# Transposed z and experts' products one piece later in the sequence, mask additions with a near due time

## The chip, the cores and the metric

The kernel runs on one core of a Trainium2 chip. The metric is the device time of one execution in microseconds (us). Of the kernel before, three timed executions and one profiled execution are at hand. The engines are named as in the profile: PE is TensorE's matmul side (PEld its weight loads), DVE is VectorE, ACT is ScalarE, POOL is GpSimd, SP is SyncE, which issues most DMAs.

## The reference, cut to what matters

A block of a transformer on x of shape (2, 1024, 1024): local attention on a convolved input, then a linear layer with four active low-rank experts and a gate.

```python
x = x + attn(layernorm(x))       # conv 3 -> q, k, v; 16 blocks of 128 tokens, 16 heads of 64
    # scores = where(causal, q k / 8, -1e9); p = softmax(scores); o = p v; o wo; @ proj_w + proj_b
xn = layernorm(x)
y = xn @ W_base.T + b_base
z = einsum(xn, A[active])                        # 4 experts, rank 8
alpha = softmax(log(prior + eps) + router(xn))   # over the 4 active experts
x = x + y + sum_e alpha_e * 2 * (z_e @ B_e)
```

## The kernel before, in words

Three stages follow each other. In the **convolution** (to about 233 us) x is normalised, transposed and convolved. In the **attention stage** (233 to about 490 us) a unit i is a pair of heads in a chunk of 512 tokens, 32 units in all, and step K of the loop (L1382) handles two of them. The **dense stage** (from about 523 us) handles the 2048 tokens in 16 pieces n of 128. The end of the attention stage, the first projections and the rounding of the dense weights overlap between 480 and 526 us; I call this the passage.

Products keep close to full precision with pairs of rounded numbers: `three` (L136 to L140) does hi x hi, hi x lo and lo x hi, so nearly all matmuls have line 140. A "hi" part is a cast on ACT, a "lo" part a subtraction on DVE.

The order of the instructions on each engine is decided when the program is built. Every operation is an `Op` (L269) with an engine, an assumed cost, a due time, a lead, operations that it comes after, and the places in pools that it needs and gives back. `trace` (L289) plays the plan: on each engine it takes, among the operations that can start, the first one by due time, and the one that can start at once before the others. An operation may start at most its lead ahead of its due time. The due time of PE's operations is the running sum of their costs (`at[0]`), in the order in which the plan's functions are called; those of other engines are set relative to it. The result is a fixed order: each engine works through its queue in order, and an instruction that waits holds up all that are queued behind it on that engine. A change of one due time can so move operations on all engines.

Names of operations, used below (i a unit, n a piece):

- Attention: Q.i, V.G.b (products for queries and keys, and values), q, v (their copies from PSUM; v with even b on ACT, L864, odd b on DVE, L862), S.i (scores, `scores`, L887), k.i (two mask additions, `masked`, L903, on DVE), x.i (maximum, L917), e.i (exponentials on ACT in two halves of four, L922), r.i (reciprocal, L929), n.i (normalisation on POOL, L933), T.i (transposed probabilities, L940), t.i (their copies, L948 on DVE and L950 on ACT), O.i (probabilities x values, L957), h.i and l.i (hi and lo of it, L971 and L978), W.i (product with wo).
- yj, yk, yl, y: steps that put together the convolved tokens on DVE (L559 to L589), which read and write SBUF.
- Dense stage: X.n loads x (L1069), POOL adds the projection's bias to it (L1072). P.n is the projection in two halves (`project`, L1074), the residual is added on DVE (L1087); then statistics (L132, L134, L1092), 1/std on POOL (L1097), normalised xn.n (L1102), TX.n (its transposition in two halves, L1109), xT.n hi and lo (L1116 on ACT, L1120 on DVE). Y.n.k.dc is a third k of the columns times one eighth dc of the rows of the weights. Columns 0 to 35 of k = 0 hold z and the router's logits; from them `plan_gate` makes the gate (L1151 to L1175) after Y.n.0.7. Z.n transposes gate x z (L1179), ACT copies it to zT (L1183), E.n.k adds the experts' products to the same banks (L1193), DVE adds them to x (L1200), and when all three thirds are added, SP stores the piece (L1206).
- Weight parts rl, wz (L1052, L1060): rounding of the dense weights on DVE in the passage.

Pools: `m` is PSUM, 8 banks, which every product from Q to Z takes (S takes two) and the copy or addition that reads it last gives back; for S it is the mask additions. `a4` (11 tiles) holds the probabilities, their transposes, oT, the x tiles, xn and xT (two tiles). A tile of it goes to the operation that asks next, the one given back longest ago first.

Around the change, the loop over the pieces (L1460) calls for n = 1 to 15: TX of n+1, P of n+2, for n = 1 the z and experts of piece 0, the first third of the columns, the gate, the second third, the last third, then z and experts of piece n itself. The last piece has its own ending. Mask additions (L1249) have a due time of 11 us before T.i of their unit, and a lead of 40 us.

Of the kernel before, what the change touches and what calls it, by code (L numbers as in the profile page):

```python
# [39 lines left out]
def preln_block_kernel(  # L40
# [592 lines left out]
    DVE, ACT, PE, DMA = "DVE", "ACT", "PE", "DMA"  # L633
# [4 lines left out]
    loaded, gs, gone = {}, {}, {}  # L638
# [69 lines left out]
    last, ready = None, {}  # L708
# [5 lines left out]
    for q, (v, n, dc) in enumerate(units):  # L714
# [6 lines left out]
        due = at[0]  # L721
# [3 lines left out]
        for i in range(2):  # L725
            d = dc + i
# [4 lines left out]
            for c in range(NCC):  # L731
                after = [last, side, ready[v, d]]
                if v == 5 and n == 0 and d == 0:
                    after.append(gone[0, max(0, c - 1)])
                last = Op(
                    PE, HALF / NCC, at[0], 6.0, after, partial(multiply_unit, q, i, c), lag=0.0
                )
# [28 lines left out]
    def product(v, d, c, side):  # L766
        after = [last, side, ready[v, d]]
        if d == 0:
            after.append(gone[v - 1 if v > 1 else 5, max(0, c - 1)])
        at[0] += HALF / 3  # L770
        return Op(
            PE, HALF / 3, at[0] - HALF / 3, 6.0, after, partial(multiply, v, d, c), lag=0.0
        )
# [7 lines left out]
    for v, dc in [(v, dc) for v in (1, 2, 3) for dc in range(0, NDC, 2)] + [(4, 0), (4, 2)]:  # L781
# [6 lines left out]
        for d in (dc, dc + 1):  # L788
            begin_chunk(v, d, at[0])
            for c in range(NCC):  # L790
                last = product(v, d, c, side)
# [14 lines left out]
    for c in range(NCC):  # L806
# [4 lines left out]
        for d in range(NDC // 2, NDC):  # L811
            last = product(4, d, c, sides[d - d % 2])
# [313 lines left out]
    def cut(n, k):  # L1126
        return (LAST_CUTS if n == len(gs) - 1 else CUTS)[k]
# [88 lines left out]
    gs = [ch * NB + b for ch in (2, 3, 0, 1) for b in range(NB)]  # L1216
    d = {}

    def pe(key, takes, after, f, lead=8.0, need=("m",), give=()):
        d[key] = Op(PE, takes, at[0], lead, [d.get(a) for a in after], f, need=need, give=give)  # L1220
        at[0] += takes
        return d[key]

    def op(key, e, takes, due, after, f, lead=14.0, **kw):
        d[key] = Op(e, takes, due, lead, [d[a] for a in after if a in d], f, **kw)
        return d[key]
# [9 lines left out]
    def plan_v(G, b):  # L1236
        ch, g = divmod(G, 2)
        pe(("V", G, b), MM, [("y", ch, 4), ("y", ch, 5)], partial(values, G, b),
           give=("t4",) * 2 if g == 1 and b == NB - 1 else ())
        op(("v", G, b), *((DVE, 0.6) if b % 2 else (ACT, 0.55)), at[0], [("V", G, b), ("v", G, 0)],  # L1240
           partial(values_out, G, b), need=("vh",) if b == 0 else (), give=("m",))
# [4 lines left out]

    def plan_softmax(i, due):
        for j in range(2):
            op(("k", i, j), DVE, 0.69, due - 11.0 + 0.7 * j, [("S", i), ("k", i, j - 1)],  # L1249
               partial(masked, i, j), need=("a4",) if j == 0 else (), give=("m",), lead=40.0)  # L1250
        op(("x", i), DVE, 1.21, due - 9.5, [("k", i, 0), ("k", i, 1)], partial(maximum, i),
           lead=40.0)
        for j in range(2):
            op(("e", i, j), ACT, 1.6, due - 8.0 + 1.6 * j, [("x", i)], partial(exponentials, i, j),
               lead=40.0)
        op(("r", i), DVE, 0.2, due - 4.0, [("e", i, 0), ("e", i, 1)], partial(reciprocal, i),
           lead=40.0)
        op(("n", i), POOL, 2.3, due - 3.7, [("r", i)], partial(normalized, i), lead=40.0)
# [9 lines left out]
    def plan_o(i):  # L1268
        pe(("O", i), 0.9, [("t", i, 0), ("t", i, 1)] + [("v", i // 4, b) for b in range(NB)],
           partial(attend, i), give=("a4",) + (("vh",) if i % 4 == 3 else ()))  # L1270
        op(("h", i), ACT, 0.6, at[0] + 1.0, [("O", i)], partial(attended_hi, i), need=("a4",))
        op(("l", i), DVE, 0.7, at[0] + 2.0, [("h", i)], partial(attended_lo, i), give=("m",))
# [15 lines left out]
    def plan_tokens(ch, c, due):  # L1288
        k = (ch, c)
        op(("yd", *k), DMA, 1.0, due - 12.0, [("W", 0)] if ch == 1 and c < 0 else [],  # L1290
           partial(tokens_load, ch, c, ml), lead=6.0, lag=3.3, need=("ml",))
        op(("yj", *k), DVE, 0.75, due - 5.0, [("yd", *k)], partial(tokens_join, ch, c, 0),
           need=("t2", "t2"))
        op(("yk", *k), DVE, 1.0, due - 4.0, [("yj", *k)], partial(tokens_join, ch, c, 1))
        op(("yl", *k), DVE, 0.95, due - 3.0, [("yk", *k)], partial(tokens_join, ch, c, 2),
           give=("ml", "t2"))
        op(("yh", *k), ACT, 0.6, due - 1.8, [("yl", *k)], partial(tokens_hi, ch, c),
           need=("t4",))
        op(("y", *k), DVE, 0.64, due - 0.8, [("yh", *k)], partial(tokens_lo, ch, c),
           give=("t2",))  # L1300
# [34 lines left out]
    def plan_tx(n):  # L1335
        g = gs[n]
        for h in range(2):
            pe(("TX", n, h), 0.44, [("xn", n)], partial(transpose_x, g, h),
               give=("a4",) if h else ())
            op(("xh", n, h), ACT, 0.55, at[0] + 0.5, [("TX", n, h), ("xh", n, 0)],  # L1340
               partial(x_hi, g, h),
               need=("a4",) * 2 if h == 0 else ())
            op(("xl", n, h), DVE, 0.65, at[0] + 1.2, [("xh", n, h)], partial(x_lo, g, h),
               give=("m",))

    def after_dense(n, k, dc):
        return [("xl", n, dc // 4), ("rl", "wb", dc, 0), ("rl", "wb", dc, 1), ("wz", dc, 1)] + (
            [("Y", n, k, dc - 1)] if dc else [])

    def plan_dense(n, k, dcs):  # L1350
        a, b = cut(n, k)
        for dc in dcs:
            pe(("Y", n, k, dc), 3 * (b - a) * 0.000454, after_dense(n, k, dc),
               partial(dense, n, k, [dc]), need=("m",) if dc == 0 else (),
               give=("a4",) * 2 if (k, dc) == (2, NDC - 1) else ())

    def plan_gate(n):
        g = gs[n]
        op(("g0", n), DVE, 0.4, at[0] + 0.5, [("Y", n, 0, NDC - 1)], partial(gate_logits, g))
        op(("g1", n), ACT, 0.3, at[0] + 1.0, [("g0", n)], partial(gate_exp, g))  # L1360
        op(("g2", n), DVE, 1.25, at[0] + 2.0, [("g1", n)], partial(gate, g))

    def plan_z(n):
        pe(("Z", n), 0.1, [("g2", n)], partial(transpose_z, gs[n]))
        op(("z", n), ACT, 0.2, at[0], [("Z", n)], partial(z_out, gs[n]), give=("m",))

    def plan_e(n, k, last):
        a, b = cut(n, k)
        pe(("E", n, k), (b - a) * 0.00046, [("z", n), ("Y", n, k, NDC - 1)], partial(experts, n, k),
           need=())  # L1370
        op(("a", n, k), DVE, 0.55, at[0] + 0.5, [("E", n, k)], partial(add_y, n, k), give=("m",))
        if last:
            op(("o", n, k), DMA, 0.7, at[0] + 1.0, [("a", n, k)], partial(store, n, k))
        elif k == 2:
            op(("o", n), DMA, 1.4, at[0] + 1.0, [("a", n, j) for j in range(3)], partial(store, n),
               lag=3.3, give=("a4",))

    PAIRS = NI // 2
    for i in range(2):
        plan_q(i)  # L1380
    pools = ["ml", "t2", "ml", "t2"]
    for K in range(PAIRS):  # L1382
        a, b = 2 * K, 2 * K + 1
# [3 lines left out]
        if K > 1:  # L1387
            for i in (a - 4, b - 4):
                plan_o(i)
        if K + 1 < PAIRS:  # L1390
            for i in (a + 2, b + 2):
# [4 lines left out]

        for v in (range(2 * (K % 2), 2 * (K % 2) + 2) if K < PAIRS - 2 else range(NB)):
            if K < PAIRS - 1:
                plan_v(K // 2, v)
# [12 lines left out]
        if K % 4 == 0 and K:  # L1412
            plan_tokens(ch - 1, 5, t0 + 6.0)
        if K == PAIRS - 4:
            op(("pb",), DMA, 1.4, t0 + 8.0, [], load_projb, lag=3.0, need=("t4",))
            op(("bb0",), DVE, 1.0, t0 + 1.0, [], load_bb, lag=5.0, need=("t4", "t4"))
            op(("bb1",), ACT, 2.3, t0 + 9.0, [("bb0",)], round_bb)
            op(("bb2",), DVE, 1.2, t0 + 12.0, [("bb1",)], finish_bb, give=("t4", "t4"))
        if K == PAIRS - 3:
            for k, (wc, h) in enumerate([(wc, h) for wc in range(NWC) for h in range(2)]):  # L1420
# [35 lines left out]
        for k in range(3):  # L1456
            plan_dense(0, k, [dc])
    plan_gate(0)
    done = 0
    for n in range(1, len(gs)):  # L1460
        last = n == len(gs) - 1

        if n + 1 < len(gs):
            plan_tx(n + 1) if n + 1 > 1 else None
        if n + 2 < len(gs):
            plan_p(n + 2)
        if n == 1:
            plan_z(0)
            for k in range(3):
                plan_e(0, k, False)  # L1470
        plan_dense(n, 0, range(NDC))
        plan_gate(n)
        plan_dense(n, 1, range(NDC))
        if not last:
            plan_dense(n, 2, range(NDC))
            plan_z(n)
            for k in range(3):
                plan_e(n, k, False)
        else:
            plan_z(n)  # L1480
            plan_dense(n, 2, range(3))
            for k in range(2):
                plan_e(n, k, True)
            plan_dense(n, 2, range(3, NDC))
            plan_e(n, 2, True)
# [72 lines left out]
```

## Time and profile before

| what | us |
| --- | --- |
| three timed executions | 785.03, 786.18, 786.32 |
| their median | 786.18 |
| the profiled execution | 783.39 |
| its span from the first to the last instruction | 781.1 |
| mean granted TensorE clock | 0.995 |
| PE busy in 500 to 540 us | 38.06 of 40 |
| PE busy in 540 to 580 us | 37.57 of 40 |
| PE busy in 620 to 660 us | 40.00 of 40 |
| DVE busy in 260 to 300 us | 39.10 of 40 |

How to read it: a line of a timeline is the start (us from the span's start), the busy time, engine, source line, operation, output<-inputs, shapes and number of instructions; in square brackets stands the idle time of the engine before it and who ended it. A line of the waits has the total, the number and the longest. Spans on POOL are rough, and PE's ends are modelled, so its work is better taken from the starts of successive matmuls. The chain of waits follows the work back from the end; its lines are start, duration and what ran.

### The profile page before, as it was taken

The numbers are of one execution on the slowest core, as the hardware profiler recorded it, in microseconds if no ns is written. First come the engines' busy times: TensorE is split into PE (matmuls) and PEld (weight loads), VectorE is DVE, ScalarE is ACT, GpSimd is POOL, SyncE is SP. The second block draws the span as 40 slices with busy tenths as digits, with TensorE's granted clock in tenths as the row PEclk, the third lists the DMA queues.
The fourth block names the chain that finished last, engine by engine and source line by source line (L and its number), as shares of the span: only waits on it lengthen the run. The fifth ranks groups of instructions, "written<-read, shape, count | busy, mean of one in ns | idle before, by whom it ended". The sixth has DMA issues, their size and how long they took to land.

```text
span 781.1 us, 13001 instructions
## 1 busy us (share of the span) xinstructions
PE 755.7 (97%) x4928; PEld 675.3 (86%) x4928; DVE 544.9 (70%) x1034; ACT 386.5 (49%) x1006; POOL 158.0 (20%) x138
## 2 busy tenths in 40 slices
PE   6999999999999999999999999999899999999995
PEld 6999978888888888888888888879899999999995
DVE  7788899889766998877786767995445544345431
ACT  6887346364836887777686977740011001010110
POOL 3224222110000311131112215231111121111100
PEclk9999999999999999999999999999999999999998
DMA  9837993994832111021032113310123212221111
GB/s 344 350 102 222 235 270 101 310 257 126 257 114 76 41 42 41 34 83 41 21 96 82 41 55 117 105 69 19 63 77 107 70 62 90 96 71 60 36 47 54
DMA packets 48118, 87.58 MB, mean 112 GB/s; under 512 B 3591, under 2 KB 22807, under 8 KB 48057
## 3 DMA queue, kind: packets, MB, share of 16 engines
q1 hardware_dynamic: 44328, 76.76, 28.6%
q0 software_dynamic: 3728, 10.00, 7.1%
q8 instruction: 38, 0.62, 0.3%
q14 instruction: 24, 0.19, 0.1%
HBM read 66.83 MB, written 19.92 MB: 111 GB/s over the span
## 4 chain that ended last, share of the span: by engine, by line
PE 62%; DVE 19%; DMA 13%; ACT 3%; issue 2%; POOL 1%; SPq 0%; ACTq 0%; DVEq 0%; POOLq 0%
PE pm L140 22%; DMA out<-xr 12%; PE pq L140 10%; PE py L140 9%; PE pw L140 4%; PE pv L140 4%; PE s L893 3%; PE po L957 3%; PE pt L940 2%; DVE lnst_b L132 2%; DVE xr L1087 2%; PE pp L140 2%; ACT p L922 2%; DVE xT L1120 1%; PE tr L385 1%
## 5 line engine op out<-in xcount | busy, mean ns | idle before, releaser
L140 PE MATMUL pm<-v,u 128*128 128x256 f32 (+1 forms) x1152 | 204.9, 339 | 5.7 <-ACT v L473 3.4
L140 PEld LDWEIGHTS pm<-v,u 128*128 128x128 f32 x1152 | 179.3, 191 | 28.9 <-ACT v L473 3.6
L140 PE MATMUL py<-wb,xT 128*128 128x354 f32 (+3 forms) x576 | 113.2, 327 | 0.0
L933 POOL TENSOR_TENSOR p<-p,rs 128x1024 f32<-128x1024 f32 x32 | 61.6, 1927 | 244.6 <-DVE rs L929 221.8
L140 PE MATMUL py<-wb_wr,xT 128*128 128x354 f32 (+3 forms) x576 | 108.8, 324 | 0.0
L922 ACT ACTIVATE p<-p,nmx 128x128 f32<-128x128 f32 x256 | 99.3, 392 | 3.5 <-DVE nmx L917 3.5
L140 PEld LDWEIGHTS py<-wb_wr,xT 128*128 128x128 f32 x576 | 96.2, 188 | 2.0
L140 PEld LDWEIGHTS py<-wb,xT 128*128 128x128 f32 x576 | 95.0, 189 | 0.2
L140 PE MATMUL pq<-yt,wqk 128*128 128x512 f32 x384 | 94.3, 399 | 0.9 <-DVE p L908 0.9
L140 PEld LDWEIGHTS pq<-yt,wqk 128*128 128x128 f32 x384 | 70.8, 188 | 19.3 <-DVE p L908 1.7
L1157 ACT ACTIVATE al<-lg,nm 128x4 f32<-128x4 f32 x16 | 4.8, 298 | 143.7 <-DVE nm L1152 143.7
L1072 POOL TENSOR_TENSOR xr<-xr,projb 128x1024 f32<-128x1024 f32 x16 | 39.1, 2443 | 165.1 <-DMA xr<-in_x 130.0
L1120 DVE TENSOR_TENSOR xT<-trx,xT 128x512 fp32r<-128x512 f32 x32 | 21.6, 686 | 44.0 <-ACT xT L1116 39.0
L922 ACT ACTIVATION_READ_ACCUMULATOR p<-p,nmx 128x1 f32 x256 | 48.9, 191 | 0.0
L140 PE MATMUL pw<-oT,wot 128*128 128x512 f32 x192 | 47.6, 396 | 0.0
L908 DVE TENSOR_TENSOR p<-s,mask 128x512 f32<-128x512 f32 x64 | 42.1, 681 | 7.2 <-PE s L893 7.1
L140 PE MATMUL pv<-wvt,yt 128*128 128x512 f32 x192 | 46.6, 392 | 0.0
L140 PEld LDWEIGHTS pw<-oT,wot 128*128 128x128 f32 x192 | 35.9, 188 | 8.6 <-DVE oT L978 0.2
L140 PEld LDWEIGHTS pv<-wvt,yt 128*128 128x128 f32 x192 | 36.1, 188 | 8.2
L1116 ACT CAST xT<-trx 128x512 fp32r<-128x512 f32 x32 | 17.7, 590 | 51.1 <-DMA out<-xr 45.5
L1200 DVE TENSOR_TENSOR xr<-py,xr 128x318 f32<-128x318 f32 (+5 forms) x48 | 23.9, 507 | 26.3 <-PE py L1193 26.3
L917 DVE TENSOR_REDUCE nmx<-p 128x8 f32<-128x1024 f32 x32 | 38.6, 1208 | 0.4
(161 smaller groups left out, 1188.2 us busy)
## 6 DMA issues: line engine op xcount, KB each, us to landing
g<-in_conv_w SPq DMA_DIRECT2D x48, 384.0 KB
mdr<-m SPq DMA_DIRECT2D x36, 256.0 KB
g<-in_conv_w POOLq DMA_DIRECT2D x24, 384.0 KB, 7.7
xt<-in_x SPq DMA_DIRECT2D x16, 512.0 KB
xr<-in_x SPq DMA_DIRECT2D x16, 512.0 KB
out<-xr SPq DMA_DIRECT2D x15, 512.0 KB
ml<-mdr SPq DMA_DIRECT2D x18, 384.0 KB
raw_wb<-in_w_base SPq DMA_DIRECT2D x16, 256.0 KB
```

The costliest lines, as they stand in the source:

```text
L132: nc.vector.bn_stats(st[:, h, :], src[:, ts(h, D // 2)])
L140: nc.tensor.matmul(ps, l[a], r[b], start=first and i == 0, stop=last and i == 2)
L893: nc.tensor.matmul(s[j][:, b, :], qh[ts(j, DH), ts(b, P)], kh[ts(j, DH), ts(b, P)], start=True, stop=True,)
L908: nc.vector.tensor_tensor(ps[i][0][:, ts(j, NB), :], ss[i][j], mask[:, None, :].to_broadcast([P, NB, P]), ALU.add,)
L917: nc.vector.tensor_reduce(nmx, p, AX.X, ALU.max, negate=True)
L922: nc.scalar.activation(p[:, k, :], p[:, k, :], AF.Exp, bias=nmx[:, k : k + 1], accum_out=sm[:, k : k + 1],)
L933: nc.gpsimd.tensor_tensor(p, p, rs[:, :, None].to_broadcast([P, 2 * NB, P]), ALU.mult)
L957: nc.tensor.matmul(po[ts(j, DH), ts(b, P)], vh[:, b, ds((i % 4) * P + j * DH, DH)], pT[:, j, ts(b, P)], start=True, stop=True,)
L1072: nc.gpsimd.tensor_tensor(xrs[g], xrs[g], pwt["b"], ALU.add)
L1116: nc.scalar.copy(xTs[g][0][:, ts(h, 4), :], trxs[g, h])
L1120: nc.vector.tensor_tensor(lo, trxs.pop((g, h)), hi, ALU.subtract)
L1200: nc.vector.tensor_tensor(x2[:, a:b], py, x2[:, a:b], ALU.add)
```

## The change

Two edits. The mask additions' due time becomes the earlier of the one before and 4 us after the due time of their scores. And z and the experts' products of piece n-1 are called in the next turn of the loop, after TX of n+1 and before P of n+2 (`plan_experts`, new); for n = 1 and for the last piece they come after the first third of the columns and its gate. The loop's unused `done = 0` goes.

```diff
     def plan_softmax(i, due):
         for j in range(2):
-            op(("k", i, j), DVE, 0.69, due - 11.0 + 0.7 * j, [("S", i), ("k", i, j - 1)],
+            op(("k", i, j), DVE, 0.69, min(due - 11.0, d["S", i].due + 4.0) + 0.7 * j, [("S", i), ("k", i, j - 1)],
                partial(masked, i, j), need=("a4",) if j == 0 else (), give=("m",), lead=40.0)
...
+    def plan_experts(n):
+        plan_z(n)
+        for k in range(3):
+            plan_e(n, k, False)
...
-        if n + 1 < len(gs):
-            plan_tx(n + 1) if n + 1 > 1 else None
+        if 1 < n + 1 < len(gs):
+            plan_tx(n + 1)
+        if 1 < n < len(gs) - 1:
+            plan_experts(n - 1)
         if n + 2 < len(gs):
             plan_p(n + 2)
-        if n == 1:
-            plan_z(0)
-            for k in range(3):
-                plan_e(0, k, False)
         plan_dense(n, 0, range(NDC))
         plan_gate(n)
+        if n == 1 or last:
+            plan_experts(n - 1)
         plan_dense(n, 1, range(NDC))
         if not last:
             plan_dense(n, 2, range(NDC))
-            plan_z(n)
-            for k in range(3):
-                plan_e(n, k, False)
```

More of the change, by code (lines that the diff above doesn't have):

```diff
@@ L1458, in preln_block_kernel @@
     plan_gate(0)
-    done = 0
     for n in range(1, len(gs)):
         last = n == len(gs) - 1
-        if n + 1 < len(gs):
-            plan_tx(n + 1) if n + 1 > 1 else None
+        if 1 < n + 1 < len(gs):
+            plan_tx(n + 1)
+        if 1 < n < len(gs) - 1:
+            plan_experts(n - 1)
         if n + 2 < len(gs):
             plan_p(n + 2)
-        if n == 1:
-            plan_z(0)
-            for k in range(3):
-                plan_e(0, k, False)
         plan_dense(n, 0, range(NDC))
         plan_gate(n)
+        if n == 1 or last:
+            plan_experts(n - 1)
         plan_dense(n, 1, range(NDC))
```

## The prediction

> **What bounds the kernel now.** I read the page's head first, then TensorE's waits by stage, then the timelines at each wait.
>
> ```profile
> PE 755.7 (97%) x4928; PEld 675.3 (86%) x4928; DVE 544.9 (70%) x1034; ACT 386.5 (49%) x1006; POOL 158.0 (20%) x138
> ```
>
> TensorE is busy for 97% of the span, so no more can be won than its idle time, 25 us. The list of waits, 320 to 540 us and then 540 us to the end, shows what of that lies where the change works (the waits before 233 us, in the convolution, aren't touched):
>
> ```profile
> PE po L957 <- DVE pT L948: 1.1, 2, 0.9
> PE trx L1109 <- DVE xT L1120: 0.8, 1, 0.8
> ...
> PE py L1193 <- ACT zT L1183: 2.4, 1, 2.4
> PE pzt L1179 <- DVE zr L1175: 1.5, 4, 0.5
> ```
>
> (total, count, longest). With the bank waits of 0.3 us at 280, 0.9 us at 318 and 0.9 us at 488 us, some 8 us can be had at most, 1%. The reader should see how little that is: an in-order TensorE at 97% loses more by one badly placed instruction than all these waits together.
>
> The wait at 550 us is not what its name says. The timeline has
>
> ```profile
> 552.55 0.58 ACT L1116 CAST xT<-trx 128x512 fp32r<-128x512 f32 x1 [5.62 <-DMA out<-xr]
> 553.03 0.27 ACT L1183 CAST zT<-pzt 98x128 fp32r<-98x128 f32 x1
> 553.35 0.41 PE L1193 MATMUL py<-bb,zT 98*128 98x318 f32 x1 [2.43 <-ACT zT L1183]
> ```
>
> zT of piece 1 is queued on ACT behind xT of piece 3, and xT's buffer is that of the x tile of piece 0, whose store must land first. The chain of waits in the dense stage repeats that every piece:
>
> ```profile
> 607.97 10.67 DMA out<-xr
> ...
> 618.72 0.59 ACT xT L1116
> ...
> 619.34 0.69 DVE xT L1120
> 620.03 0.43 DVE xr L1200
> 620.47 0.60 DVE xT L1120
> 621.06 1.20 DVE xr L1087 x2
> 622.26 1.20 DVE lnst_b L132 x2
> ...
> 623.80 0.52 DVE xr L1200
> ...
> 624.41 10.55 DMA out<-xr
> ```
>
> Store, xT, DVE's work, next store: 16.4 us. TensorE's own work for a piece, by starts of successive matmuls in the timeline, is 24 products of 0.486, two transposes of 0.44, two projections of 1.39, three experts' products of 0.16 and the transposed z of 0.06: 15.9 us. So TensorE gains 0.5 us on the chain with each piece, until from piece 8 on it waits for z (the four waits above).
>
> **The masks.** 64 additions (0.68 us on DVE, from PSUM) keep their number and length and move a few places ahead. Where DVE was free they ran soon after the scores anyway, so most of the sequence is as before: built, the order of TensorE's operations differs before 490 us in two swaps only, at nothing, since both neighbours were ready. Three places matter.
> - At 318 us a product waited 0.9 us (1.1 with the restart) for a bank that a late mask addition held. In the new order that addition precedes the token sums: minus 1.1.
> - At 263 us, scores of pair 5 wait for the bank that DVE's copy of v (V.0.3) frees, now behind a mask addition and two token sums more: 263.02 becomes about 263.45, plus 0.4.
> - Near 297 us, ACT now runs the exponentials in another order, and DVE puts the copies l.2 and l.3 and two reciprocals ahead of the maximum of pair 6. r.4 waits for ACT until 289, POOL's normalisation (1.9 us) follows and holds up the token step behind it, and the maximum ends at 293.2 instead of 288.0. Three halves of exponentials (1.6 each) then stand ahead of ACT's copy v.1.2: 298.6 instead of 295.1. Scores of pair 8 were due at 297.5 and need that bank: plus 1.1. Before, its spare was 2.4 us.
> Sum of the stage: plus 0.4; bounds minus 1.4 (no new wait) to plus 2.
>
> **The passage to the dense stage, 490 to 526 us.** This is the dearest part, and neither the diff nor a due time shows it: since the planner sees banks and DVE differently, the transposes of piece 0 (TX.0) now stand ahead of P.2.0, W.28, W.29 and T.30, T.31, where they stood behind them.
>
> ```profile
> 506.28 0.64 DVE L1087 TENSOR_TENSOR xr<-pp,xr 128x512 f32<-128x512 f32 x1
> 506.33 0.57 POOL L1097 TENSOR_TENSOR lnrs_b<-lnve_b,mhalf 128x1 f32<-128x1 f32 x1 [9.41 <-DVE lnve_b L1092]
> 506.89 4.20 POOL L933 TENSOR_TENSOR p<-p,rs 128x1024 f32<-128x1024 f32 x2
> 508.26 1.06 DVE L1102 TENSOR_SCALAR xn<-xr,lnmv_b,lnrs_b 128x1024 f32<-128x1024 f32 x1
> 512.07 0.49 PE L1109 MATMUL trx<-identr,xn 128*128 128x128 f32 x3
> ```
>
> TX.0 needs xn.0. TensorE reaches the new place at 506.1. DVE's work ahead of the statistics of piece 0 is the same set in both orders (masks and weight parts change places), so they end at 506.4 again; POOL's rstd at 507.0; then xn.0, now ahead of l.28 and l.29. But POOL goes straight on to the normalisation of pair 30. Here a rule and a row differ. The Trainium skill, "SBUF — State Buffer", section "SBUF: two separate sides", says that DVE's two-port modes and GpSimd lock a port pair for a whole instruction and the loser blocks fully. The row: xn took 1.06 instead of 0.80 with POOL's row running, so 0.26 lost, but it came late in POOL's instruction. By the rule, coming at its start, it waits for some 1.65 us, ends at 509.5, and TensorE stands for 3.5 us. If nothing blocked, xn would end at 507.9: 2.0 us. I take the lock, because nearer rows show the full price: DVE's 0.19 us wz took 1.76 us at 515.08 beside POOL's x plus bias.
>
> Queued behind TX.0 are P.2.0, W and T: 6.9 us of work, so T.31 ends its turn at 516.9 (0.4 more for a bank from ACT). Before, O.30 ran at 514.0. Now its copy t.30 stands on DVE behind three weight parts: from xn.0 at 509.5, r.31 0.2, l.28 and l.29 1.4, residual 0.6, weight part 0.7 (POOL's next normalisation in the way), 0.1, statistics 1.7, weight part 0.7 make 515.0; then wz is blocked by POOL's 2.4 us addition until 517.4, rl 0.6, t.30 0.7: 518.7. TensorE waits 1.9. O.30, O.31, P.2.1, TX.1.0, W.30 and W.31, TX.1.1 take 7.1: the dense stage starts at 525.8 where it was 522.75: **plus 3.1**. The waits of before (1.1, 0.4, 1.0) go, but their place is taken. With no lock at xn the same sum gives plus 1.6; the upper bound is 4. Spare of DVE after 529 us (4 us idle) lets the last weight parts be in time.
>
> **z and the experts' products.** Same instructions, fewer or no more waits on zr: between the last gate product and Z lie 5.25 us (odd pieces) or 3.3, where gate and z on DVE and ACT take 2.75. So the 2.2 us of waits for zr vanish, and at piece 1 TensorE has done three products (1.46 us) more before it stands for zT: its wait falls from 2.6 to 1.1. But what is late next? In the new ACT order z(n) stands behind xT(n+2) for every piece; before, from piece 4 on, it stood ahead. So the store is now in a loop with TensorE: E(n).0 to P(n).1's end 2.68, 0.18 to DVE, residual 0.61, then statistics 1.63 (even pieces; in odd ones they follow the add), add and issue 0.58: 5.68 even, 4.05 odd; store to xT 10.69 (mean of six rows), xT and zT to the product 0.80. Two pieces: 5.68 + 4.05 + 2 x 11.49 = 32.7 us, against 2 x 15.86 = 31.7 of TensorE's. The wait is 0.3 and 0.65 us by turns from piece 2 to 12, starting at once, not from piece 8: with 1.1 at piece 1 and half a us more at piece 12 (both halves of xT ahead of z) 6.2 to 6.5, against 4.9 before: **plus 1.4**. Bounds: minus 4.7 (store shorter by 0.5: no wait at all) to plus 3 (0.15 more per turn). SP's queue keeps its order but for one load of a weight part, which moves one place up, far ahead of its use; X of piece n+4 follows the store as before, and POOL's queue is unchanged. At nothing, while the loads land 15 us after issue and are used a piece later.
>
> **Sum.** 0.4 + 3.1 + 1.4 = 4.9; the profiled execution took 783.39 (781.1 span and 2.3 around it), so 788.3 on its scale; the median of the runs is 786.18, so 791.0. I round the least certain term, the masks', down and say 790.8.
>
> **Rivals.**
> - *The store stays out of the way* (faster). Place: E(n).0. If store and xT take under 11.0 us rather than 11.49, the two-piece loop is under TensorE's 31.7, and z moved later takes away all dense waits: -4.7, masks -1.1, passage +3.1: -2.7, 783.5. For it: Z's waits do go. Against: six store rows between 10.63 and 10.75. Chance 0.07.
> - *Nearly nothing*: no lock at xn (+1.6), masks -1.1, dense 0: +0.5, 786.7. For it: most of the order is as before. Against: TX.0's place. Chance 0.13.
> - *More*: masks at +2, passage +4, dense +3: 795. For it: DVE is full at 260 to 300 and 480 to 526 us, where every shift meets POOL. Chance 0.17.
> - The forecast, 788.5 to 793: 0.63.
>
> Under 0.2% (1.6 us) this kernel's measurement can't tell a change from none. Faster 0.07, same 0.13, slower 0.80. Range: 786.4 to 794.0; it takes in half the "nearly nothing" case and the lower part of "more".
>
> **What would show it.** Right: a wait of 3 to 4 us of trx for xn near 506 us; one of about 2 us of po for pT near 517; py L1193 waiting for zT in nearly every piece, pzt for zr in none; the wait of pq for p at 318 gone. Wrong: trx without a wait (xn written before 506, so DVE was ahead), or experts' products that never wait (the store isn't in TensorE's loop).

## The result, and the profile after

The changed kernel takes 789.88 us (median of eight executions, 788.65 to 791.24) against 786.56 us for the kernel before in the same session: a ratio of 1.0044, 95% interval 1.0026 to 1.0062, which is 2.0 to 4.9 us more. The forecast was 790.8 us, 4.6 above the median it started from. The sum came out; two of its terms did not.

The profiled execution of after took 791.15 us (span 789.3, granted clock 0.986, where before had 0.995). Its first page, and its waits of TensorE from 320 to 540 us and from 540 us to the end (total, count, longest):

```profile
PE 761.4 (96%) x4928; PEld 680.4 (86%) x4928; DVE 546.2 (69%) x1034; ACT 385.2 (49%) x1006; POOL 156.8 (20%) x138
```

```profile
PE trx L1109 <- DVE xn L1102: 3.0, 1, 3.0
PE pt L940 <- ACT qk L883: 1.6, 1, 1.6
PE pt L940 <- ACT pT L950: 0.3, 1, 0.3
```

```profile
PE py L1193 <- ACT zT L1183: 3.7, 7, 1.0
```

In before the list from 233 to 340 us had one line, and in after it is empty:

```profile
PE pq L140 <- DVE p L908: 0.9, 1, 0.9
```

So the bank wait of pq at 318 us is gone. A wait of the transposes for xn is new, the wait for zT at one piece has become seven (ten, with those too short for the list), and none is left for zr. Three of the four signs named in the forecast are there; the fourth, po waiting for pT near 517 us, is not.

Single profiles must be read with care here. I profiled the kernel before a second time, expecting its dense stage within 1 us of the first; it took 1.2 us more, in the same order. So I matched every operation of every run to its counterpart in the first profile of before. The table gives how much longer each stage took than there, in us. The stages are cut at the first product Q.0.0, the last V.7.3, the first dense product Y.0.0.0, the last expert's product E.15.2 and the end of the span.

| run | convolution | attention | passage | dense | end | ratio of times [95%] |
| --- | --- | --- | --- | --- | --- | --- |
| before again | +1.5 | 0.0 | +0.1 | +1.2 | -0.1 | - |
| after | +3.5 | -2.3 | +3.0 | +2.2 | +1.8 | 1.0044 [1.0026, 1.0062] |
| masks alone | +1.5 | -2.4 | +2.3 | +1.7 | +0.4 | 0.9994 [0.9974, 1.0015] |
| z alone | +3.3 | 0.0 | +0.7 | +1.9 | +1.9 | 1.0045 [1.0033, 1.0057] |
| TX.0 back | +1.8 | -2.3 | +0.8 | +2.3 | +1.8 | 1.0006 [0.9988, 1.0024] |
| n.30 after xn.0 | +1.6 | -2.3 | +0.3 | +2.4 | +1.9 | 1.0017 [1.0005, 1.0029] |
| TensorE kept busy | -0.1 | -2.3 | +0.7 | +2.2 | +1.9 | 1.0010 [0.9992, 1.0028] |
| z 14 early | +1.6 | -2.4 | +2.3 | +2.4 | -0.4 | 1.0001 [0.9988, 1.0013] |
| z ahead of xT | -0.1 | -2.3 | +2.7 | -4.0 | +1.8 | 0.9956 [0.9938, 0.9975] |
| after, 12 buffers | +3.3 | -2.5 | +2.3 | -4.7 | +2.5 | 0.9952 [0.9932, 0.9972] |
| masks, 12 buffers | +2.8 | -2.5 | +2.3 | -4.5 | -0.5 | 0.9915 [0.9886, 0.9944] |
| best | -0.2 | -2.4 | +0.9 | -4.2 | -0.5 | 0.9907 [0.9886, 0.9928] |
| two exchanges | +1.6 | -0.4 | +1.5 | +1.5 | -0.1 | - |

The convolution has the same order in all of them, so its 3.5 us are the execution's own and no part of the change. The attention stage repeats within 0.1 us from run to run. In the four runs with the old place of TX.0 and the old passage (before twice, z alone, two exchanges) the passage spreads over 1.5 us. In the four with the old dense stage (before twice, masks alone, two exchanges) that stage spreads over 1.7. Against the means of those runs the change is -2.3 in the attention stage, +2.5 in the passage (3.0 less 0.6), +1.1 in the dense stage (2.2 less 1.1) and +1.8 at the end: +3.1 us, which agrees with the times.

**Where the spread comes from.** The granted clock in the second profile of before, around the wait for zT at piece 1 (columns: stretch, its length, busy time of PE, PEld, DVE, ACT, POOL, PEclk, DMA share, GB/s):

```profile
550.00:553.00 3.00, 2.44 (x13) 1.85 (x11) 0.00 (x0) 0.00 (x0) 0.00 (x0) 1.00 0.26 96
553.00:556.00 3.00, 1.21 (x7) 1.21 (x8) 1.39 (x3) 1.24 (x3) 0.00 (x0) 0.95 0.25 104
556.00:560.00 4.00, 4.00 (x15) 3.44 (x15) 2.05 (x5) 0.00 (x0) 0.87 (x1) 0.61 0.09 37
560.00:564.00 4.00, 4.00 (x27) 4.00 (x26) 2.81 (x7) 0.00 (x0) 2.07 (x2) 1.00 0.07 15
```

TensorE stood for 2.36 us. About 1 us after it had resumed, at 555.7, the clock went to 0.5 until 559.1: 3.4 us in which only half as many products run (15 in 4 us, then 27). That costs 1.6 us on top of the wait. The first profile of before stood there for 2.43 us and kept its clock. The kernels with masks alone and with the two exchanges lost it as the second one did. The convolution shows the same step at 115 to 120 us, behind a stall of 1.8 to 1.9 us at 113 us that all 14 profiles have and that ten of them follow with half clock. Here is the clock in the first and second profile of before:

```profile
115.00:120.00 5.00, 4.69 (x21) 3.88 (x22) 4.90 (x6) 3.90 (x6) 1.04 (x2) 1.00 1.10 268
```

```profile
115.00:120.00 5.00, 4.86 (x14) 3.85 (x15) 4.90 (x6) 3.46 (x5) 1.04 (x2) 0.66 0.99 206
```

Q.0.0 starts at 233.2 us in the four runs without this stretch, at 234.8 to 235.1 in six runs with it, and at 236.1 to 236.8 in the four that also have a longer stretch of half clock near 20 us. So the first stage takes one of three lengths, 1.6 us apart.

Why is one stall of 2.43 us free, and one of 1.9 us not? In each profile the stretches of half clock begin whole multiples of 3.413 us apart: in after at 19.05, 118.04, 510.57 and 780.22 us, which is 29, 115 and 79 such lengths. So I cut each profile into windows of 3.413 us on that grid, and took TensorE's idle time in each from 30 us to the last product. All 19 stretches of half clock follow a window with 1.83 to 2.66 us idle. Of the 3016 other windows one has more than 1.8 us (1.87). So what counts is the idle time within one window, and the limit is a little over half of it. In the first profile of before the border fell into the stall: 0.94 us of it lie in one window and 1.49 in the next. In the second, 2.35 us lie in one. The four stalls at 113 us that went free are of both kinds: two were divided (1.48 and 1.51 us in the fuller window), two lay at the limit (1.78 and 1.87).

### The profile page after: what moved, and what is told of

The parts are those of the page before. It is cut to its first block, busy times and chain, and to the rows that moved or that the text cites. A ratio compares the mean times of both kernels' runs of the same rounds, so it can differ in the third digit from the quotient of the medians.

```text
span 789.3 us, 13007 instructions
## 1 busy us (share of the span) xinstructions
PE 761.4 (96%) x4928; PEld 680.4 (86%) x4928; DVE 546.2 (69%) x1034; ACT 385.2 (49%) x1006; POOL 156.8 (20%) x138
## 4 chain that ended last, share of the span: by engine, by line
PE 78%; DMA 11%; DVE 5%; ACT 2%; issue 2%; POOL 0%; ACTq 0%; SPq 0%; POOLq 0%; DVEq 0%
PE pm L140 26%; PE py L140 13%; PE pq L140 11%; DMA out<-xr 11%; PE pw L140 5%; PE pv L140 5%; PE s L893 4%; PE pp L140 4%; PE po L957 3%; PE pt L940 3%; PE tr L385 2%; PE idle L702 1%; PE py L1193 1%; PE trx L1109 1%; DVE xr L1087 1%
## 5 line engine op out<-in xcount | busy, mean ns | idle before, releaser
L140 PE MATMUL pm<-v,u 128*128 128x256 f32 (+1 forms) x1152 | 207.6, 342 | 5.2 <-ACT v L473 3.1
L140 PEld LDWEIGHTS pm<-v,u 128*128 128x128 f32 x1152 | 181.5, 194 | 29.0 <-ACT v L473 3.4
L445 DVE TENSOR_TENSOR u<-g,u 128x768 fp32r<-128x768 f32 x40 | 37.5, 953 | 2.9 <-ACT u L441 2.6
```

Source lines behind the costliest of these rows:

```text
L140: nc.tensor.matmul(ps, l[a], r[b], start=first and i == 0, stop=last and i == 2)
L445: nc.vector.tensor_tensor(lo, raws.pop((v, dc)), hi, ALU.subtract)
```

## The experiments

### 1. Each edit alone: masks, z

Masks alone is before with the first hunk of the diff only; z alone is before with the rest only.

```diff
# masks alone, on before
-            op(("k", i, j), DVE, 0.69, due - 11.0 + 0.7 * j, ...
+            op(("k", i, j), DVE, 0.69, min(due - 11.0, d["S", i].due + 4.0) + 0.7 * j, ...
# z alone, on before: plan_experts and its two calls, as in the change
```

> The kernel before with the near due time of the masks alone; z and the experts' products stay where they were. The planned order then has TX.0 ahead of P.2.0, so the due time alone would bring it. Theory (from the two traces): the stage of the attention up to V.7.3 gains 2.3 us (0.97 at the bank wait at 318 us, 0.7 where two query-key products no longer stand between two score or attention products, 0.4 + 0.3 near S.5 and S.8), the passage from 490 to 526 us loses 3.0: +0.7 us against before, a ratio of 1.001, with a TX wait of about 3 us for xn and no change from Y.0.0.0 on. Rival 1, the prediction's steps: stage +0.4, passage +3.1: +3.5 us, 1.0045. Rival 2, the moved z brings TX.0 forward: then no wait for xn here and -2.3 us, 0.997.

> The kernel before with z and the experts' products one piece later and the masks' due time left as it was. The operations up to the dense stage are those of before. Theory: experts' products wait for zT in nearly every piece (5 to 6 us in all), the waits of pzt for zr (1.5) and of P.3.1's neighbour (2.4) go: +2.2 us from Y.0.0.0 to the end, as in the trace of after, ratio 1.0028. The prediction's sum says +1.4 (1.0018). Rival: the dense stage's loss in the after trace is that execution's lower clock (0.986 against 0.995) and no wait: then within 0.5 us of before.

Masks alone: 0.9994, -2.0 to +1.2 us. The prediction's +3.5 for this half lies outside; the theory's +0.7 is within. The wait of trx for xn is there (2.7 us), so the due time alone brings TX.0 forward. Z alone: 1.0045, 2.6 to 4.5 us more, above the theory's +2.2 and the prediction's +1.4. The rival (clock only) falls. The missing part stood in no view that I had read for the dense stage: it comes after the last product (experiment 6).

### 2. TX.0 back

After, with the near due time withheld from the last two units.

```diff
-            op(("k", i, j), DVE, 0.69, min(due - 11.0, d["S", i].due + 4.0) + 0.7 * j, ...
+            op(("k", i, j), DVE, 0.69, (min(due - 11.0, d["S", i].due + 4.0) if i < 30 else due - 11.0) + 0.7 * j, ...
```

> The changed kernel with the near due time withheld from the masks of the last two pairs (30 and 31) alone. The planned order then puts TX.0 behind T.31, and P.2.0 behind TX.0; everything before pair 30 and the dense stage are as in after. Theory: the wait of trx for xn (3.0 us) goes and the passage costs what it did before: 3 us less than after, so about -0.1 us against before (ratio 1.000). Rival: the passage is bound by DVE and POOL, not by TX.0's place: with P.2.0 late, O.30 or P.2.1 waits instead, and no more than 1 us comes back (ratio 1.003).

1.0006: 3.0 us less than after by the medians' ratios (give or take 1.4 each), 2.2 less in the passage by the traces. The attention stage keeps its -2.3. So four mask additions of 64, those of units 30 and 31, put TX.0 in its costly place. Other waits came up instead (pw for oT 1.0, trx for xT 1.3), of the kind that the rival named, but more came back than the 1 us that it allowed.

### 3. The lock at xn, and what the stall costs beyond itself

In after, xn.0 on DVE and n.30 on POOL start within 0.1 us of each other:

```profile
508.03 0.57 POOL L1097 TENSOR_TENSOR lnrs_b<-lnve_b,mhalf 128x1 f32<-128x1 f32 x1 [9.42 <-DVE lnve_b L1092]
508.58 1.88 POOL L933 TENSOR_TENSOR p<-p,rs 128x1024 f32<-128x1024 f32 x1
508.64 2.38 DVE L1102 TENSOR_SCALAR xn<-xr,lnmv_b,lnrs_b 128x1024 f32<-128x1024 f32 x1
...
511.08 1.97 PE L1109 MATMUL trx<-identr,xn 128*128 128x128 f32 x8 [3.02 <-DVE xn L1102]
...
512.70 2.22 PE L140 MATMUL pp<-pw,oh 128*128 128x512 f32 x6
```

xn takes 2.38 us. Two things are to be told apart: is that the lock, and why do the transposes and products behind it take so long (eight transposes 1.97 us, six products 2.22)? The clock answers the second:

```profile
506.00:508.00 2.00, 2.00 (x10) 1.35 (x8) 1.93 (x7) 2.00 (x12) 0.00 (x0) 1.00 0.64 215
508.00:510.00 2.00, 0.06 (x1) 0.00 (x0) 1.98 (x3) 2.00 (x8) 1.97 (x2) 1.00 0.38 125
510.00:512.00 2.00, 0.92 (x5) 0.92 (x6) 2.00 (x4) 1.29 (x3) 1.16 (x2) 0.64 0.25 86
512.00:514.00 2.00, 2.00 (x8) 1.80 (x8) 2.00 (x5) 1.17 (x2) 1.20 (x1) 0.50 0.23 88
514.00:516.00 2.00, 2.00 (x10) 1.61 (x10) 1.93 (x5) 0.00 (x0) 0.44 (x1) 1.00 0.42 142
```

PEclk is 0.5 from 510.6 to 514.0; the window before it, 507.2 to 510.6, has 2.51 us of the stall. Whether the stall brought it on is tried below.

```diff
# n.30 after xn.0: the order of issue of two operations, on after
+    behind[d["r", NI - 2]] = d["xn", 0]
+    behind[d["n", NI - 2]] = d["xn", 0]
# TensorE kept busy: 20 transposes of the identity ahead of TX.0, on after
-        for c in range(4):
-            nc.tensor.transpose(pt[:, c, :], xns[g][:, ts(4 * h + c, P)], ident)
+        for c in [-1] * (20 * (h == 0 and g == gs[0])) + list(range(4)):
+            nc.tensor.transpose(pt[:, max(c, 0), :], xns[g][:, ts(4 * h + c, P)] if c >= 0 else ident, ident)
```

> The changed kernel with the reciprocal of pair 30, which releases POOL's normalisation n.30, one place later on DVE: behind xn.0 and not ahead of it. Nothing else moves. Theory (DVE's xn and POOL's two-input multiplication shut each other out): xn.0 then takes 0.8 instead of 2.4 us, the wait of trx for xn falls from 3.0 to 1.4 us, n.30 ends 1 us later, which nothing waits for (T.30 comes 4 us after it): 1.6 us less than after, ratio to before about 1.0024. Rival 1 (xn.0 is slow for a reason of its own, such as its place after xp.0): no change, 1.0044. Rival 2: the later n.30 and n.31 hold up POOL's xp.1 and x plus bias, and a later wait (T.30, O.30 or P.2.1) takes it back.

> The changed kernel with 20 idle transposes of the identity ahead of TX.0, into the bank that TX.0 then overwrites (extra work; no result changes). They need nothing but that bank, so TensorE works for some 2.2 us of the 2.5 to 3.2 us in which it stood for xn.0. In every profile in which it stood for 2.35 us or more (before once excepted, 2.43) the granted clock fell to a half for 3.4 us afterwards, and the products of P.2.0 and W.28 took 0.43 instead of 0.22 us each: 1.6 us beyond the wait. Theory (the idleness halves the clock): with the filling the half clock near 510 us is gone and the same products end 1.6 us earlier, ratio to before about 1.0024 against 1.0044 of the changed kernel. Rival (the half clock comes of something else at that time, such as the transfers of the weight parts, which take a quarter of the DMA engines there): it stays, and the time is that of the changed kernel or, with the transposes in the way, more.

With n.30 one place later the timeline reads

```profile
505.65 0.57 POOL L1097 TENSOR_TENSOR lnrs_b<-lnve_b,mhalf 128x1 f32<-128x1 f32 x1 [9.41 <-DVE lnve_b L1092]
506.26 0.81 DVE L1102 TENSOR_SCALAR xn<-xr,lnmv_b,lnrs_b 128x1024 f32<-128x1024 f32 x1
506.99 0.26 DVE L929 RECIPROCAL rs<-sm 128x8 f32<-128x8 f32 x2
507.13 1.09 PE L1109 MATMUL trx<-identr,xn 128*128 128x128 f32 x8 [1.71 <-DVE xn L1102]
507.33 3.76 POOL L933 TENSOR_TENSOR p<-p,rs 128x1024 f32<-128x1024 f32 x2 [1.11 <-DVE rs L929]
```

xn takes 0.81 us, so the other 1.57 were POOL's instruction: the lock, tested by one exchange. (The weight part that now meets POOL's next normalisation, at 509.26, takes 2.38 us in its turn.) TensorE stands for 1.7 instead of 3.0 us, and at 1.7 the clock stays: the eight transposes take 1.09 us, not 1.97. The passage is 2.7 us shorter than in after and the ratio 1.0017, about the 1.6 us less expected plus the clock that the expectation had left out; a wait of O.30 (0.7 us) takes part of it back.

Kept busy, TensorE ran at full clock over the same stretch, and the ratio is 1.0010:

```profile
506.00:508.00 2.00, 1.09 (x9) 1.09 (x10) 2.00 (x4) 1.45 (x4) 1.17 (x2) 1.00 0.26 92
508.00:510.00 2.00, 2.00 (x10) 1.62 (x10) 2.00 (x5) 0.73 (x2) 1.03 (x1) 1.00 0.25 98
510.00:512.00 2.00, 2.00 (x10) 1.57 (x9) 1.93 (x7) 0.00 (x0) 0.60 (x1) 1.00 0.46 137
512.00:514.00 2.00, 2.00 (x19) 1.67 (x17) 1.81 (x4) 0.59 (x1) 2.00 (x2) 1.00 0.37 132
```

xn was as slow as in after (2.39 us), and the DMA share in the stall as high (0.39 in 504 to 506 us); TensorE still stood for 1.46 us, and only its idleness was changed. So idleness is what halves the clock, the rival (transfers) falls, and useless work in a stall is worth having. By stages the filling gains 2.3 us on after and 1.6 to 2.1 on the three other runs that have the same passage (masks alone, z 14 early, z ahead of xT). The Trainium skill, "TensorE: Matmul & The Clock Gate", section "What's actually happening", tells of such half-rate stretches and of a free-running window of about 3.4 us. The length agrees (3.413 us here), and so does the free running: the stretches keep to one grid through a whole profile. It puts the fall after at least one idle window, which would leave a wait of 2.4 us free. Here a window idle for a little over half of it was enough (1.83 us or more in all 19 cases), and 1.71 us, the stall with n.30 one place later, were not: the measurement decides.

### 4. The store's loop in the dense stage

Two ways to break it: one more 4 KB buffer in `a4`, or z ahead of xT on ACT.

```diff
# after, 12 buffers
-    A4 = NHP + 3
+    A4 = NHP + 4
-        zr = zrs[g] = small.tile([P, ZK], FR, tag="zr", name=f"zr_{g}")
+        zr = zrs[g] = small.tile([P, ZK], FR, tag="zr", name=f"zr_{g}", bufs=2)
# z ahead of xT, on after
         if 1 < n < len(gs) - 1:
             plan_experts(n - 1)
+            d["xh", n + 1, 0].after.append(d["z", n - 1])
```

> The changed kernel with 12 instead of 11 of the 4 KB buffers that x, xn, xT, the probabilities and their transposes share (paid for by two instead of four buffers of the row zr). TensorE's order is the same. With one more buffer xT(n+2) gets that of a piece whose store has landed long before, so xT is no longer behind the store. Theory (store, xT, z is the loop): the waits of the experts' products for zT, 5.3 us in all, vanish and nothing takes their place: 5.3 us less than after, ratio against before about 0.998. Rival 1 (the order on ACT alone makes z late, xT stands there for TX, not for the store): the waits stay, same as after, 1.0044. Rival 2 (another link comes next, DVE's adds and the residual): half comes back, 1.001.

> The changed kernel with z(n) ahead of xT(n+2) on ACT, for pieces 1 to 13; TensorE's order is untouched, and on DVE only the second half of xT(n+2) moves behind two of the adds. Theory: what TensorE waits for in the dense stage is z standing behind xT's wait for the store; with z ahead, the waits of the experts' products for zT (5.3 us) go, and the store's loop on DVE (10.7 store, 1.2 two copies on ACT, then 0.7 and 0.6 xT, 0.6 and 0.6 residual, 1.5 adds, 0.1; 1.65 statistics in every second piece: 16.0 to 16.8 a piece) has its whole spare left and asks nothing of TensorE before the last pieces: 4 to 5 us less than after, ratio to before 0.998 to 1.000. Rival: the store's loop is longer than TensorE's 15.9 us a piece wherever z stands, and TensorE waits for zr or a bank instead: at most 2 us less than after, 1.002 or more.

In after the chain of waits goes the way that the forecast drew; every piece has the store, xT, z, the expert's product, the residual, the add, and the next store:

```profile
593.35 10.69 DMA out<-xr
...
604.14 0.04 ACT xT L1116
604.18 0.44 issue
604.62 0.28 ACT zT L1183
...
604.95 0.41 PE py L1193
...
607.93 0.69 DVE xr L1087
...
610.17 0.53 DVE xr L1200
...
610.76 10.59 DMA out<-xr
```

Either cure takes all those waits away: the dense stage is 6.9 us (buffer) and 6.2 us (order) shorter than in after, and the ratios are 0.9952 and 0.9956, both faster than before. With twelve buffers the list of TensorE's waits from 540 us on is empty, and with the buffer the build even puts z behind both halves of xT on ACT. So z's place on ACT costs nothing of itself; it costs when xT ahead of it waits for a store. Both rivals fall: the order alone is not the cause, and the store's loop on DVE takes nothing back. Both gains were larger than the 5.3 us expected. By starts of products the waits come to 5.5 us, and the ten products behind them take 0.41 us each instead of 0.31: 6.5 us in all.

### 5. What the later z is worth once the store is out of the way

Before with the masks' due time and twelve buffers, z in its old place (the first diff of experiment 1 and the first of experiment 4).

> The due time of the masks and the twelfth 4 KB buffer, with z and the experts' products where they were before: beside the changed kernel with twelve buffers it tells what the later place of z is worth once the store is out of the loop. Theory: the waits for zr (1.5 us) and for zT at piece 1 (2.4 us) came of the store as well, so they go with the buffer, and the later z gives nothing more: the same time as with z moved and twelve buffers (0.995 of before) within 1 us. Rival: z(n) in its own piece has too little time (gate and z take 2.75 us, 3.3 us between), waits of 0.3 to 0.5 us stay in most pieces, and the later z is worth 3 us or more with the buffer: 0.999.

0.9915, against 0.9952 with z moved (the intervals overlap slightly). The dense stages are equal within 0.2 us (-4.5 and -4.7): without the store neither order waits (but for 0.3 us for zr in the old one), so the later z gains nothing there. What remains is the end, -0.5 against +2.5, which is the next experiment.

### 6. The end of the kernel

In after, z and the experts of piece 14 come behind the gate of piece 15, so that the store of piece 14 is issued at 772.0, beside those of piece 15. The moved place for all pieces but the first:

```diff
-        if 1 < n < len(gs) - 1:
+        if 1 < n:
             plan_experts(n - 1)
...
-        if n == 1 or last:
+        if n == 1:
             plan_experts(n - 1)
```

> The changed kernel with z and the experts' products of piece 14 at the start of piece 15, as those of the other pieces, and not behind its gate. In the changed kernel the store of piece 14 (512 KB) is issued at 772.0, 7 us before the last one, and the span ends 11.25 us after the last expert's product; in before it ends 9.43 us after it. Theory: the last stores share the queue with that late store; 8 us earlier it is out of the way: 1.8 us less than after, ratio 1.0021, with 9.4 us behind the last product. Rival: the end is 11.25 us for another reason (the order of the last three stores): no change, 1.0044.

1.0001, 3.4 us less than after by the ratios (give or take 1.0 and 1.4), 2.2 less at the end by the traces. The stretches after the last products, first in after (E.15.2 at 778.05), then with piece 14 early (E.15.2 at 775.6); the last two columns are DMA share and GB/s:

```profile
774.00:778.00 4.00, 4.00 (x29) 3.94 (x28) 1.02 (x2) 0.27 (x1) 0.00 (x0) 1.00 0.23 50
778.00:782.00 4.00, 0.33 (x3) 0.12 (x1) 0.53 (x2) 0.00 (x0) 0.00 (x0) 0.78 0.26 92
782.00:786.00 4.00, 0.00 (x0) 0.00 (x0) 0.00 (x0) 0.00 (x0) 0.00 (x0) 0.50 0.24 90
786.00:789.30 3.30, 0.00 (x0) 0.00 (x0) 0.00 (x0) 0.00 (x0) 0.00 (x0) 0.50 0.06 22
```

```profile
766.00:770.00 4.00, 4.00 (x24) 4.00 (x23) 0.64 (x3) 0.00 (x0) 0.00 (x0) 1.00 0.14 37
770.00:774.00 4.00, 4.00 (x29) 3.94 (x28) 1.15 (x8) 0.66 (x3) 0.00 (x0) 1.00 0.24 63
774.00:778.00 4.00, 1.88 (x15) 1.67 (x14) 1.45 (x3) 0.00 (x0) 0.00 (x0) 1.00 0.20 62
778.00:782.00 4.00, 0.00 (x0) 0.00 (x0) 0.00 (x0) 0.00 (x0) 0.00 (x0) 0.89 0.26 82
782.00:784.60 2.60, 0.00 (x0) 0.00 (x0) 0.00 (x0) 0.00 (x0) 0.00 (x0) 0.50 0.08 28
```

In after the queue is busy for 8 us from E.15.2 on at a share of about 0.25. It still has 0.79 MB to move there, of which a part is piece 14; with piece 14 early it is 0.55 MB, as in before. At the 82 to 92 GB/s of these rows the difference takes some 2.6 to 2.9 us (an estimate), and 2.2 were gained: the span ends 11.25 us after E.15.2 in after, 9.0 us here. This is the term that the forecast lacked.

### 7. Two exchanges on TensorE

Before with only the exchanges that the masks' due time brings to TensorE's order; nothing moves on DVE.

```diff
+    behind[d["Q", 18, 0]] = d["S", 17]
+    behind[d["Q", 26, 0]] = d["O", 21]
```

> The kernel before with only TensorE's two exchanges: Q.18.0 behind S.17 instead of between S.16 and S.17, and Q.26.0 behind O.21 instead of between O.20 and O.21. Read by starts of operations, which agree within 0.02 us between executions in this stage. Theory (a query-key product between two score or attention products costs a restart of each): S.16 to S.20 is 0.38 and S.24 to S.28 0.32 us shorter than in before, without any change on DVE. The prediction's step (at nothing): 0.0. Rival: the 0.7 us came of the order of the masks, then 0.0 here too, and it stays with the due time.

S.16 to S.20 is 0.20 us shorter and S.24 to S.28 0.21, so the exchanges gain 0.4 of the 0.7 us; the other 0.3 needs the masks' order on DVE. Neither the theory nor the prediction (at nothing) was exact.

### 8. The parts joined

Before with the near due time for units 0 to 29 and twelve buffers.

> The kernel before with the near due time for all masks but those of pairs 30 and 31, and the twelfth 4 KB buffer; z where it was. It joins what each run has shown: TX.0 behind T.31 (2 to 3 us less than with TX.0 early), and the store out of TensorE's loop (0.9915 with TX.0 early). Theory: the two add, 0.988 to 0.990 of before, 777 to 778 us. Rival: with DVE full at 490 to 526 us the place of TX.0 gains nothing beside the buffer: 0.9915.

779.41 us, ratio 0.9907, 0.9886 to 0.9928: faster than both kernels, by 5.7 to 9.0 us against before, and at the edge of the 0.988 to 0.990 expected. By the traces the passage is 1.4 us shorter than with TX.0 early; by the times the two versions with twelve buffers can't be told apart (0.9907 and 0.9915), so that the gains add is shown in the stages only. Its waits from 540 us on, where before had five:

```profile
PE pzt L1179 <- DVE zr L1175: 0.7, 1, 0.7
```

## Why the prediction was right, step by step

**Masks, plus 0.4: wrong in sign.** The attention stage gained 2.3 us. The minus 1.1 at 318 us came (-1.0). The two losses did not. Between S.5 and O.1, at 263 to 265 us, it was 0.4 us shorter instead of longer. Near 297 us the chain of maximum, exponentials and v.1.2 was built on one assumption, that POOL's normalisation holds up the token step: in after that step (`yt`, on DVE) started 0.2 us ahead of POOL's instruction and was not held up, so the maximum ended in time and S.8 did not wait:

```profile
291.28 0.64 DVE L589 TENSOR_TENSOR yt<-y,yt 128x512 fp32r<-128x512 f32 x1
291.51 4.03 POOL L933 TENSOR_TENSOR p<-p,rs 128x1024 f32<-128x1024 f32 x2 [13.39 <-ACT qk L883]
```

And "at nothing" for the two exchanges should have been minus 0.4.

**Passage, plus 3.1: right in size, in its first half also in cause.** The early place of TX.0, the lock at xn and the stall were as told (2.3 to 3.0 us measured in six profiles, 3.5 forecast). What followed was not: O.30 did not wait 1.9 us for its copy. POOL's rstd of piece 1 took 0.94 us, so the addition queued behind it, which was to block the small weight part, started at 516.49, after that part (516.02). This is read from the trace; no run tested that order by itself. In its place stood the half clock, 1.6 us, of which the forecast says nothing. That a wait of 1.9 us was replaced by a loss of 1.6 is luck. Against the mean of the undisturbed passages the change cost 2.5.

**Dense stage, plus 1.4: right in mechanism, in size partly by luck.** The loop, the seat of the waits and their turn of 0.3 and 0.65 us (in after 0.20 to 0.33 and 0.63 to 0.97, by starts of products, from piece 3 to 11) are as forecast, and the waits for zr went. Against the mean of four old dense stages it is +1.1; against the one profile that the forecast had, +2.2. That profile was the one of four without the half clock at piece 1. After has none there either, with a wait of only 1.0 us at piece 1. Beside the three other profiles the later z thus also saves the half clock's 1.6 us, a term that the forecast left out. Of the +2.2 the waits themselves make 0.6 (5.5 against 5.0 us in all); the restarts behind them take some of the rest, since an expert's product took 0.41 us after a wait and 0.31 without one, and how the remainder divides stays open.

**The end, at nothing: missed.** Plus 1.8 us. The forecast followed the queue of SP while it was in the loop, and not past the last product, though the diff gives the last piece an ending of its own.

Together: 4.9 forecast, 3.1 by the stages, 3.3 by the times. A loss of 2.7 us too much in the attention stage, one of 1.8 us not seen at the end: the closeness of the total is in part luck, and only experiments with one part at a time show it. Of the rivals, "the store stays out of the way" was right about what it would be worth (its dense waits gone) and wrong about whether it would.

## What to carry to other kernels

When TensorE is busy for 97% of the span, cost each new wait that can fill half of a 3.4 us window (here 1.8 us or more) with the half clock behind it, and look whether idle work can fill it. Follow a transfer that a change makes later to its landing, above all the last one. When the order stems from a planner, look for what it moves far from the edit: four due times here took back what the other sixty gained.

## What the runs showed of the hardware that I had not expected

- Half clock for 3.4 us (1.6 us lost) followed each of the 12 windows of 3.413 us in which TensorE was idle for 1.89 us or more, 7 of the 8 with 1.83 to 1.87 us, and none with 1.78 us or less. The windows keep to one grid through an execution, so the same stall is free in one execution and dear in the next: 2.43 us went free where the border of two windows fell into it.
- The same stretches make the unchanged convolution take 233.2, about 235 or about 236.5 us. Without such a stretch, the attention stage repeats within 0.1 us, so a comparison by starts of operations resolves what the total time can't.
- Which of two instructions, on DVE and on POOL, is first by 0.1 to 0.2 us decides 1.6 us at xn.0. The same is seen near 487 us, in a part that was not touched: in the first profile of before DVE's weight part started at 485.55, ahead of POOL's addition at 485.75, and took 0.68 us; in the second it started at 487.67, behind POOL's at 487.50, took 2.75 us, and TensorE waited 1.5 us that it had not waited before. The whole passage took the same in both.
